# Attention b of a two-attention layer stack: how the row maxima are placed into the queries, and when the other work runs beside it

## The chip, the cores and the metric

The kernel runs on one core of one Trainium2 chip. TensorE (PE) multiplies matrices and transposes; its weight loads are listed apart (PEld). VectorE (DVE), ScalarE (ACT) and GpSimd (POOL) do the elementwise work, and SyncE (SP) issues every transfer, in order, from one queue. The metric is the device time in microseconds. An instruction's line is given as L781 and so on.

## The reference, cut to what matters

Two batches of 512 positions with 512 features pass through four residual layers. All of it is float32.

```python
x = x + attn_a(layernorm(x))      # 32 heads of 128, 8 key/value heads, int4-style weights
x = x + ffn(layernorm(x))         # 8 low-rank experts, two of them chosen per position
x = x + attn_b(layernorm(x))      # 32 heads of 16, 8 key/value heads
x = x + ffn(layernorm(x))         # the same weights as before

# attn_b
q, k = rope(q), rope(k)
att = einsum(q, k) / sqrt(16)                  # per head, (512, 512)
att = where(causal, att, -inf)
probs = softmax(att)                           # needs each row's maximum
out = (probs @ v) @ Wo
```

## The kernel before, in words

Attention a and the first expert layer of batch 0 come first. The change is in what follows, attention b, with the expert layers of both batches running beside it.

**Pairs and steps.** Attention b handles two heads at a time, a *pair*; there are 32 pairs, 16 for each batch. For every pair two generators run. `maxima` (L742) computes the scores with rows on partitions (`sc_b`, L758), adds the causal mask and reduces each row to its maximum on DVE (L762). `probabilities` (L789) computes the scores again, transposed (`st_b`, L805), takes exp on ACT (L811) and clears the upper triangle on POOL (L814). Each has three *steps* per pair: `sc_b` in the order 128+256, 512, 384 columns, and `st_b` as 512, 384, 128+256. `probabilities` runs LEAD = 8 steps behind `maxima`. Pair p has its first maxima step at step 3p.

**How the maximum gets subtracted.** Queries and keys are split into a high and a low float32r part and laid out so that one matmul over 64 partitions gives the whole product. The maximum is appended as two more partitions, 64 and 65: the keys hold -1 there and the queries the maximum's high and low part. So when `maxima` runs, these rows have to be zero, and before `probabilities` runs they have to hold the maxima. Before the change this is done as follows. POOL clears the two rows of a query buffer (L740) when it is loaded again. After the last reduction of a pair, POOL splits the maxima of each head into `mm` (L770, L771), four small operations. `maxima_in` (L776) transposes `mm` on PE into `tpm` (L781, four matmuls), and ACT copies two rows to each head's half of the query buffer (L784, two copies).

**Where the queries come from.** `queries_halved` (L724) splits the queries of four pairs on ACT and POOL into `hl`, and `spread` (L707) writes it twice to DRAM (L711). `queries_in` (L735) loads one pair's 64 rows from there into one of five query buffers (L738). Keys go the same way (`keys_in`, L718).

**The order of the work.** The main loop (L926 on) writes out PE's order by hand: each step places at most one `maxima_in`, one step of `probabilities`, one of `maxima`, two of the products with the values (`num_b`, L831) when they are due, and then side work. The order on the other engines, SP among them, is planned from dependences while the program is built. All `sc_b`, `st_b` and `tpm` tiles share five PSUM buffers, in turn.

**Side work and its pace.** Side work is a chain of generators that yield their cost in units of about one microsecond of PE (0.9 for a 512-column float32 matmul, MM, L157). Each step adds `pace` to a budget and runs side work until the budget is spent. A generator may yield a larger number to hold the work back: `norm_parts` (L158) yields 7.0 between a layer norm's statistics and its transposes. In the first half of the loop the side work is the end of the first expert layer of batch 1 (`py_f`) and batch 1's projections (`pkv_b`, `pq_b`, and the transposes `pxT_b`, `tpk`, `tpq`); in the second half it is the output projection of batch 0 (`po`, L887), the second expert layer of batch 0 and then `po` of batch 1. After the loop the rest of batch 0's second expert layer, the last `po` and the second expert layer of batch 1 run alone. The last `po` waits for the softmax denominators, which pass through DRAM (`dens_b`, `rb_b`).

Of the kernel before, what the change touches and what calls it, by code (L numbers as in the profile page):

```python
# [11 lines left out]
F32 = mybir.dt.float32  # L12
I32 = mybir.dt.int32
F32R = mybir.dt.float32r
AF = mybir.ActivationFunctionType
ALU = mybir.AluOpType
# [3 lines left out]
P = 128  # L20
B, S, DM = 2, 512, 512
# [10 lines left out]
B_NH, B_NKV, B_HD = 32, 8, 16  # L32
# [8 lines left out]
def kernel(  # L41
# [21 lines left out]
    nc = tc.nc  # L63
# [27 lines left out]
    order = const.tile([P, NE], F32, tag="order", name="order")  # L91
# [66 lines left out]
    def norm_parts(b, which):  # L158

        var = small.tile([P, NT, 2], F32, tag="mv", name=f"mv_{which}_{b}")  # L160
        for t in range(NT):
            st = small.tile([P, 6], F32, tag="st", name=f"st_{which}_{b}_{t}")
            nc.vector.bn_stats(st, x[b, t])
            nc.vector.bn_aggr(var[:, t, :], st)
        std = small.tile([P, NT], F32, tag="std", name=f"std_{which}_{b}")
        nc.scalar.activation(std, var[:, :, 1], AF.Sqrt, bias=eps)
        rstd = small.tile([P, NT], F32, tag="rstd", name=f"rstd_{which}_{b}")
        nc.vector.reciprocal(rstd, std)
        yield 7.0
        xT = place("xT", [P, NC, S], f"xnT_{which}_{b}")  # L170
        for t in range(NT):
            xn = place("xn", [P, DM], f"xn_{which}_{b}_{t}")
            nc.vector.tensor_scalar(
                xn, x[b, t], var[:, t, 0:1], rstd[:, t : t + 1], ALU.subtract, ALU.mult
            )
            pt = place("bank", [P, NC, P], f"pxT_{which}_{b}_{t}")
            for c in range(NC):
                nc.tensor.transpose(pt[:, c, :], xn[:, ts(c, P)], ident)
            nc.scalar.copy(xT[:, :, ts(t, P)], pt)
            yield MM  # L180
        return xT
# [98 lines left out]
    with ExitStack() as actx:  # L280
# [221 lines left out]
        for n in range(len(units) + 4):  # L502
# [7 lines left out]
            if at(3):  # L510
                g, b, h, nm = at(3)
# [4 lines left out]
            if at(0):  # L516
                g, b, h, nm = at(0)
# [8 lines left out]
            if at(4):  # L526
                g, b, h, nm = at(4)
                turn.append(output(wo[g], h, g * A_G + h, b, *ats.pop((g, b, h)), nm))
            if at(2):
                g, b, h, nm = at(2)  # L530
# [32 lines left out]
    for sp in range(4):  # L563
        for par in range(2):
            at = sp * STRIP + par * B_HD
# [6 lines left out]

    HALF, HM = P // 2, P // 2 + 2
    NQ = 5
    qs = [w2.tile([P, 2, S], F32, tag=f"qs{n}", name=f"qs_{n}") for n in range(NQ)]
    ks = [w2.tile([P, 4, S], F32, tag=f"ks{n}", name=f"ks_{n}") for n in range(2)]
# [6 lines left out]
    for pad in (*ks, *qs, *vpads, *(mm.bitcast(F32) for mm in mmp)):  # L585
        nc.gpsimd.memset(pad, 0.0)
    for pad in ks:
        nc.gpsimd.memset(pad[HALF:HM], -1.0)
    for pad in vpads:
        for t in range(NT):  # L590
            for kh in range(2):
# [4 lines left out]
    bp = ctx.enter_context(tc.tile_pool(name="b", bufs=1))  # L596
    hp = ctx.enter_context(tc.tile_pool(name="hT", bufs=1))
    hlp = ctx.enter_context(tc.tile_pool(name="hl", bufs=1))
    dram = ctx.enter_context(tc.tile_pool(name="dram", bufs=2, space=bass.MemoryType.DRAM))
    ptp = ctx.enter_context(tc.tile_pool(name="pT2", bufs=5))  # L600
    ps_x = ctx.enter_context(tc.tile_pool(name="ps_x", bufs=5, space=PSUM))
    ps_n = ctx.enter_context(tc.tile_pool(name="ps_n", bufs=1, space=PSUM))
# [30 lines left out]
    qTs, khls = {}, {}  # L633
# [65 lines left out]
    STEPS, LEAD = 3, 8  # L699
# [4 lines left out]

    def spread(hl, nm, order):  # L707

        to = dram.tile([4, P, S], F32, tag=f"spread{nm[0]}", name=f"spread_{nm}")
        for twice in range(2):  # L710
            nc.sync.dma_start(  # L711
                to[order[twice]].rearrange("n r s -> r n s"), hl.bitcast(F32)
            )
        return to.rearrange("n (d h) s -> (n d) h s", h=B_NKV)

    kparts, qparts = {}, {}

    def keys_in(b, kh):  # L718

        if kh == 0:  # L720
            kparts[b] = spread(khls[b], f"k_{b}", (slice(0, 4, 2), slice(1, 4, 2)))
        nc.sync.dma_start(ks[kh][:HALF], kparts[b][:, ts(kh, 4), :])

    def queries_halved(p):  # L724

        b, kh, g, _ = pairs[p]
        hl = hlp.tile([P, 2, S], F32R, tag="hl", name=f"hl_{p}")
        src = qTs[b][:, kh * 2 + g // 2, :]
        nc.scalar.copy(hl[:, 0, :], src)
        nc.gpsimd.tensor_tensor(hl[:, 1, :], src, hl[:, 0, :].bitcast(F32), ALU.subtract)  # L730
        to = spread(hl, f"q_{p}", (slice(0, 2), slice(2, 4)))
        for n in range(4):
            qparts[p + n] = to

    def queries_in(p):  # L735
        _, _, g, pr = pairs[p]
        q = qs[p % NQ]
        nc.sync.dma_start(q[:HALF], qparts.pop(p)[:, ts((g % 2) * 2 + pr, 2), :])  # L738
        if p >= NQ:
            nc.gpsimd.memset(q[HALF:HM], 0.0)  # L740

    def maxima():  # L742

        for p, (b, kh, g, pr) in enumerate(pairs):
            q, k = qs[p % NQ].bitcast(F32R), ks[kh].bitcast(F32R)
            top = small.tile([P, NT, 2], F32, tag="top", name=f"top_{p}")
            for tiles in ((0, 1), (3,), (2,)):
                sc = [
                    ps_x.tile([P, S], F32, tag="x", name=f"sc_b_{p}_{tiles[0]}_{h}")
                    for h in range(2)  # L750
                ]
                parts, at = [], 0
                for i in tiles:
                    n = (i + 1) * P
                    parts += [(i, n, h, sc[h][:, at : at + n]) for h in range(2)]
                    at += n
                for i, n, h, part in parts:
                    nc.tensor.matmul(  # L758
                        part, q[:, h, ts(i, P)], k[:, pr * 2 + h, :n], start=True, stop=True
                    )  # L760
                for i, n, h, part in parts:
                    nc.vector.tensor_tensor_reduce(  # L762
                        part, part, tri[:, S - n :], 1.0, -3e38, ALU.add, ALU.max,
                        top[:, i, h : h + 1],
                    )
                if tiles == (2,):
                    mm = mms[p] = mmp[p % len(mmp)]
                    for h in range(2):
                        at = (1 - h) * HALF
                        nc.gpsimd.tensor_copy(mm[:, :, at], top[:, :, h])  # L770
                        nc.gpsimd.tensor_tensor(  # L771
                            mm[:, :, at + 1], top[:, :, h], mm[:, :, at].bitcast(F32), ALU.subtract
                        )
                yield

    def maxima_in(p):  # L776

        mm = mms.pop(p).bitcast(F32)
        tp = ps_x.tile([P, S], F32, tag="x", name=f"tpm_{p}")
        for t in range(NT):  # L780
            nc.tensor.transpose(tp[:HM, ts(t, P)], mm[:, t, :], ident)  # L781
        for h in range(2):
            at = (1 - h) * HALF
            nc.scalar.copy(qs[p % NQ][HALF:HM, h, :].bitcast(F32R), tp[at : at + 2, :])  # L784


    due = []
# [115 lines left out]
    def parts(stage, n):  # L903
        for _ in range(n):
            next(stage, None)
# [7 lines left out]
    for kh in range(2):  # L913
        keys_in(0, kh)
# [7 lines left out]
    half = total // 2  # L922
    banks[:], homes["we"] = BESIDE, (wep, "we")
    side = chain(later, projections(1))
    pace, left = 1.05, 0.0
    for step in range(total + LEAD):  # L926
        with tc.manual_schedule(engines={mybir.EngineType.PE}):
            if step == half - 8:
                run(side)
                keys_in(1, 0)  # L930
            if step == half - 4:
                side = output_b(0, (0, 1))
                pace, left = 0.38, 0.0
            if step == half + LEAD:
                keys_in(1, 1)
            if step == half + LEAD + 10:
                side = chain(side, output_b(0, (2, 3)), experts(0, "f2", True))
                pace, left = 1.05, 0.0
            if step == total - 6:
                side = chain(output_b(1, (0, 1)), side)  # L940
                pace, left = 1.5, 0.0
            quotients[:] = [q for q in quotients if next(q, None) is not None]
            p, at = divmod(step + 4, STEPS)
            if at == 0 and p % 4 == 3 and p + 1 < len(pairs):
                queries_halved(p + 1)
            if at == 0 and 2 <= p < len(pairs):
                queries_in(p)
            p, at = divmod(step - 4, STEPS)
            if at == 0 and 0 <= p < len(pairs):
                maxima_in(p)  # L950
            if LEAD <= step:
                next(ps)
            if step < total:
                next(ms)

            if len(due) > 1 and due[1][0] <= step:
                for _ in range(2):
                    weighted_b(*due.pop(0)[1])
            left += pace
            while left > 0:  # L960
                got = next(side, None)
                if got is None:
                    left = 0.0
                else:
                    left -= got
# [2 lines left out]
        weighted_b(*due.pop(0)[1])  # L968

    run(*quotients)  # L970
    parts(side, 12)
    run(output_b(1, (2, 3)))
    homes["we"] = ptp, f"pT{S}"
    run(side, experts(1, "f2", True))
# [90 lines left out]
```

## Time and profile before

| | |
|---|---|
| median of 3 runs | 1115.84 us (1114.67 to 1116.47) |
| the profiled execution's own time | 1118.32 us |
| its span, first to last instruction | 1116.6 us |
| granted TensorE clock, mean | 0.985 |
| attention b's loop, first score to the end of its last steps | 807 to about 1052 us |
| PE, DVE, ACT, POOL busy | 95%, 77%, 55%, 53% |

In the profile a group's row has the line, engine, operation, what it writes and reads, its shape and its count; then the busy time and the mean of one, and after the next bar the engine's idle time just before it and what ended that. A timeline row has start, duration, engine, line and operation, and in brackets the idle time before. A row of windows has, for each stretch, the busy time and the number of instructions of PE, PEld, DVE, ACT and POOL, then the granted clock (1.00 is full speed), the share in which the DMA engines are busy, and GB/s. PE's busy time contains waiting inside a stream of matmuls, so 95% is not PE at its peak.

### The profile page before, as it was taken

How to read it: one execution, taken by the hardware profiler on the slowest of the kernel's cores; microseconds unless marked ns; L12 is line 12 of the kernel's file. 1: busy time of each engine (PE TensorE's matmuls, PEld its weight loads, DVE VectorE, ACT ScalarE, POOL GpSimd, SP SyncE). 2: the span in 40 equal slices, each digit the busy share in tenths (PEclk: the TensorE clock that was granted, in tenths of full speed). 3: DMA queues.
4: the chain of work that ended last, by engine and by line, in shares of the span. 5: the costliest groups of instructions: out<-in, count | busy, mean ns of one | idle time of the engine just before them, and what ended most of it. 6: DMA issues, size and time to landing. Idle time of an engine off the chain costs nothing.

```text
span 1116.6 us, 16186 instructions
## 1 busy us (share of the span) xinstructions
PE 1065.4 (95%) x4940; PEld 712.1 (64%) x4940; DVE 863.6 (77%) x2175; ACT 616.9 (55%) x1421; POOL 587.4 (53%) x916
## 2 busy tenths in 40 slices
PE   5799999999999999999999999999989999999988
PEld 3467677777777777777777777555467555555534
DVE  6889899999999999999999889573376667667142
ACT  3556566566566566566556665513166667575410
POOL 2556556656756756756656666261245566454200
PEclk9899999999999999999999999999989999889999
DMA  7301010021010010010121000043342245211010
GB/s 288 114 1 38 1 38 24 16 76 51 26 39 5 34 38 5 35 38 1 39 76 38 1 1 1 1 153 85 96 135 82 60 143 146 57 47 34 21 44 38
DMA packets 23270, 60.47 MB, mean 54 GB/s; under 512 B 4368, under 2 KB 5328, under 8 KB 20368
## 3 DMA queue, kind: packets, MB, share of 16 engines
q1 hardware_dynamic: 23184, 59.44, 16.4%
q8 instruction: 40, 0.66, 0.2%
q14 instruction: 46, 0.38, 0.1%
HBM read 45.53 MB, written 12.85 MB: 52 GB/s over the span
## 4 chain that ended last, share of the span: by engine, by line
PE 79%; DVE 10%; ACT 3%; POOL 3%; issue 2%; DMA 2%; SPq 0%; ACTq 0%; DVEq 0%; POOLq 0%
PE av L429 11%; PE sc L396 10%; PE tp L424 5%; PE ps_o L439 5%; PE ps_o L438 5%; PE ps_q L358 5%; PE ph_f L207 5%; PE ps_q L359 4%; PE py_f L266 4%; PE num_b L831 4%; PE st_b L805 3%; PE sc_b L758 3%; PE pq_b L678 2%; PE po L887 2%; DVE r_q L365 2%
## 5 line engine op out<-in xcount | busy, mean ns | idle before, releaser
L404 ACT ACTIVATE p<-sc,nmx 128x128 f32<-128x128 f32 (+3 forms) x256 | 135.7, 530 | 95.5 <-DVE nmx L399 92.7
L376 POOL TENSOR_TENSOR r_q<-r_q,tab 128x512 f32<-128x512 f32 x64 | 82.5, 1288 | 190.9 <-DVE rs_q L375 190.9
L396 PE MATMUL sc<-kT,qT 128*128 128x128 f32 (+3 forms) x512 | 180.2, 433 | 0.9 <-POOL qT L377 0.9
L365 DVE SCALAR_TENSOR_TENSOR r_q<-ps_q,s_q,r_q 128x512 f32<-128x512 f32 x192 | 143.5, 748 | 37.3 <-PE ps_q L359 23.5
L413 POOL TENSOR_SCALAR p<-p,rden 128x128 f32<-128x128 f32 (+3 forms) x256 | 140.2, 561 | 59.1 <-DVE rden L411 20.7
L425 ACT COPY pT<-tp 128x128 f32<-128x128 f32 (+3 forms) x256 | 109.4, 428 | 104.4 <-PE tp L424 103.8
L762 DVE CUSTOM_DVE_ANT_0 sc_b<-sc_b,tri 128x128 f32<-128x128 f32 (+3 forms) x256 | 119.6, 517 | 51.9 <-PE sc_b L758 44.7
L429 PE MATMUL av<-pT,v 128*128 128x512 f32 (+3 forms) x512 | 148.5, 433 | 0.0
L429 PEld LDWEIGHTS av<-pT,v 128*128 128x128 f32 x512 | 97.0, 190 | 80.2 <-issue 53.9
L448 DVE SCALAR_TENSOR_TENSOR acc<-ps_o,s_o,acc 128x512 f32<-128x512 f32 x186 | 137.4, 739 | 5.5 <-PE ps_o L439 5.4
L399 DVE CUSTOM_DVE_ANT_0 sc<-sc,tri 128x128 f32<-128x128 f32 (+3 forms) x256 | 125.3, 490 | 8.0 <-PE sc L396 7.1
L358 PE MATMUL ps_q<-xh,w_q 128*128 128x512 f32 x256 | 123.9, 484 | 7.4 <-DVE r_q L365 7.3
L424 PE MATMUL tp<-ident,p 128*128 128x128 f32 x640 | 113.1, 273 | 2.6 <-POOL p L413 2.6
L811 ACT ACTIVATE pT_b<-st_b 128x384 f32<-128x384 f32 (+1 forms) x192 | 90.5, 528 | 40.4 <-PE st_b L805 39.4
L396 PEld LDWEIGHTS sc<-kT,qT 128*128 128x128 f32 x512 | 96.0, 189 | 24.8 <-POOL qT L377 1.3
L438 PE MATMUL ps_o<-ah,w_o 128*128 128x512 f32 x256 | 107.9, 422 | 1.7 <-DVE acc L448 1.0
L439 PE MATMUL ps_o<-al,w_o 128*128 128x512 f32 x256 | 104.9, 410 | 3.4 <-DVE al L152 3.4
L424 PEld LDWEIGHTS tp<-ident,p 128*128 128x128 f32 x640 | 83.1, 141 | 30.6 <-issue 6.4
L359 PE MATMUL ps_q<-xl,w_q 128*128 128x512 f32 x256 | 102.0, 398 | 0.0
L814 POOL TENSOR_SCALAR_AFFINE_SELECT pT_b<-pT_b 128x128 f32<-128x128 f32 (+1 forms) x192 | 62.9, 338 | 64.2 <-ACT pT_b L811 61.7
L377 POOL TENSOR_TENSOR qT<-r_q,rs_q 128x512 f32<-128x512 f32 x64 | 85.3, 1333 | 1.0
L446 POOL TENSOR_TENSOR acc<-acc,part 128x512 f32<-128x512 f32 x62 | 79.7, 1286 | 10.1 <-ACT part L445 10.1
(179 smaller groups left out, 2048.6 us busy)
## 6 DMA issues: line engine op xcount, KB each, us to landing
codes_q<-in_q_codes_dram SPq DMA_DIRECT2D x8, 1024.0 KB
codes_o<-in_o_codes_dram SPq DMA_DIRECT2D x8, 1024.0 KB
spread_q<-hl SPq DMA_DIRECT2D x16, 512.0 KB
qs<-spread_q SPq DMA_DIRECT2D x32, 256.0 KB
x_a<-in_x_dram SPq DMA_DIRECT2D x8, 256.0 KB
codes_k<-in_k_codes_dram SPq DMA_DIRECT2D x2, 1024.0 KB
codes_v<-in_v_codes_dram SPq DMA_DIRECT2D x2, 1024.0 KB
x_r<-in_x_dram SPq DMA_DIRECT2D x8, 256.0 KB
```

What stands on the lines that cost most here:

```text
L358: nc.tensor.matmul(ps, w[:, c, ts(h, A_HD)], xh[b][:, c, :], start=True, stop=False)
L359: nc.tensor.matmul(ps, w[:, c, ts(h, A_HD)], xl[b][:, c, :], start=False, stop=True)
L365: nc.vector.scalar_tensor_tensor(r, ps, s, r, ALU.mult, ALU.add)
L396: nc.tensor.matmul(sc[:, :n], qT[:, ts(i, P)], kT[:, :n], start=True, stop=True)
L399: nc.vector.tensor_tensor_reduce(sc[:, :n], sc[:, :n], tri[:, S - n :], -(A_HD**-0.5), 3e38, ALU.add, ALU.min, nmx,)
L404: nc.scalar.activation(pr, sc[:, :n], AF.Exp, bias=nmx, scale=-1.0, accum_out=den[:, i % 2 : i % 2 + 1],)
L413: nc.gpsimd.tensor_scalar(prs[j], prs[j], rden[:, j % 2 : j % 2 + 1], 1.0, ALU.mult, ALU.mult)
L424: nc.tensor.transpose(tp[:, j, :], prs[i][:, ts(j, P)], ident)
L429: nc.tensor.matmul(av[:, j * P :], v[:, j, :], pT[:, j, j * P :], start=(j == 0), stop=(j == NT - 1))
L438: nc.tensor.matmul(ps, w[:, h, ts(n, P)], ah, start=True, stop=False)
L439: nc.tensor.matmul(ps, w[:, h, ts(n, P)], al, start=False, stop=True)
L448: nc.vector.scalar_tensor_tensor(to, ps, s, to, ALU.mult, ALU.add)
```

## The change

The maxima take four partitions instead of two (HM is 68 instead of 66): high and low part of both heads. The keys of even heads have -1 in the first two of these rows and 0 in the others, those of odd heads the reverse. Thus one cast and one subtraction on POOL split both heads, and one copy on ACT puts all four rows under both heads. A query load brings 68 rows: the four at the end of each DRAM buffer are written once with zeros, so that POOL no longer clears anything. The DRAM buffers are two for the queries and one for the keys, made once. `maxima_in` comes one step later. The norm's hold falls from 7.0 to 3.0, the paces change, the first queries of batch 1 are split at step 44 with the first keys instead of at 41, and after the loop 16 yields of side work instead of 12 run ahead of the last `po`.

```diff
@@ norm_parts
-        yield 7.0
+        yield 3.0
@@
-    HALF, HM = P // 2, P // 2 + 2
+    HALF, HM = P // 2, P // 2 + 4
...
-        nc.gpsimd.memset(pad[HALF:HM], -1.0)
+        for h in range(2):
+            nc.gpsimd.memset(pad[HALF:HM, h : 4 : 2, :], -float(h))
+            nc.gpsimd.memset(pad[HALF : HALF + 2, h : 4 : 2, :], h - 1.0)
...
-    def spread(hl, nm, order):
-        to = dram.tile([4, P, S], F32, tag=f"spread{nm[0]}", name=f"spread_{nm}")
-        for twice in range(2):
-            nc.sync.dma_start(
-                to[order[twice]].rearrange("n r s -> r n s"), hl.bitcast(F32)
-            )
-        return to.rearrange("n (d h) s -> (n d) h s", h=B_NKV)
+    kspread = dram.tile([HALF * B_NKV, S], F32, tag="kspread", name="kspread")
+    qspread = [
+        dram.tile([HM * B_NKV, S], F32, tag=f"qspread{n}", name=f"qspread_{n}") for n in range(2)
+    ]
+    for to in qspread:
+        nc.sync.dma_start(to[HALF * B_NKV :], qs[0][: (HM - HALF) * B_NKV, 0, :])
+
+    def spread(to, hl, parts):
+        to = to[: HALF * B_NKV].rearrange("(n r) s -> n r s", r=P)
+        for part in parts:
+            nc.sync.dma_start(to[part].rearrange("n r s -> r n s"), hl.bitcast(F32))
+
+    def spread_heads(to):
+        return to.rearrange("(r h) s -> r h s", h=B_NKV)
@@ queries_in
-        q = qs[p % NQ]
-        nc.sync.dma_start(q[:HALF], qparts.pop(p)[:, ts((g % 2) * 2 + pr, 2), :])
-        if p >= NQ:
-            nc.gpsimd.memset(q[HALF:HM], 0.0)
+        at = (g % 2) * 2 + pr
+        nc.sync.dma_start(qs[p % NQ][:HM], spread_heads(qspread[p // 4 % 2])[:, ts(at, 2), :])
@@ maxima
-                    for h in range(2):
-                        at = (1 - h) * HALF
-                        nc.gpsimd.tensor_copy(mm[:, :, at], top[:, :, h])
-                        nc.gpsimd.tensor_tensor(
-                            mm[:, :, at + 1], top[:, :, h], mm[:, :, at].bitcast(F32), ALU.subtract
-                        )
+                    high, low = mm[:, :, HALF:HM:2], mm[:, :, HALF + 1 : HM : 2]
+                    nc.gpsimd.tensor_copy(high, top)
+                    nc.gpsimd.tensor_tensor(low, top, high.bitcast(F32), ALU.subtract)
@@ maxima_in
-        for h in range(2):
-            at = (1 - h) * HALF
-            nc.scalar.copy(qs[p % NQ][HALF:HM, h, :].bitcast(F32R), tp[at : at + 2, :])
+        both = tp[HALF:HM].unsqueeze(1).to_broadcast([HM - HALF, 2, S])
+        nc.scalar.copy(qs[p % NQ][HALF:HM].bitcast(F32R), both)
@@ the loop
-    pace, left = 1.05, 0.0
+    pace, left = 0.8, 0.0
...
-            if step == half - 8:
+            if step == LEAD:
+                pace = 0.95
+            if step == half - 4:
                 run(side)
                 keys_in(1, 0)
-            if step == half - 4:
+                queries_halved(len(pairs) // 2)
                 side = output_b(0, (0, 1))
-                pace, left = 0.38, 0.0
+                pace, left = 0.37, 0.0
...
                 side = chain(side, output_b(0, (2, 3)), experts(0, "f2", True))
-                pace, left = 1.05, 0.0
+                pace, left = 0.95, 0.0
             if step == total - 6:
                 side = chain(output_b(1, (0, 1)), side)
-                pace, left = 1.5, 0.0
+                pace, left = 1.4, 0.0
...
-            if at == 0 and p % 4 == 3 and p + 1 < len(pairs):
+            if at == 0 and p % 4 == 3 and p + 1 < len(pairs) and p + 1 != len(pairs) // 2:
                 queries_halved(p + 1)
...
-            p, at = divmod(step - 4, STEPS)
+            p, at = divmod(step - 5, STEPS)
             if at == 0 and 0 <= p < len(pairs):
                 maxima_in(p)
@@ after the loop
-    parts(side, 12)
+    parts(side, 16)
```

## The prediction

> **What bounds the kernel now.** I read the page's shares first, then its clock row. All times are from the profiled execution's start.
>
> ```profile
> PE 1065.4 (95%) x4940; PEld 712.1 (64%) x4940; DVE 863.6 (77%) x2175; ACT 616.9 (55%) x1421; POOL 587.4 (53%) x916
> ...
> PEclk9899999999999999999999999999989999889999
> ```
>
> PE (TensorE) is busy 95% of the span, and the chain that ended last runs 79% over it. The clock row dips in slices 30, 35 and 36, all in attention b. The changed lines run after 740 us, so I cut attention b into stretches: first steps, side work in the first half, few side units, second half. The columns are busy time of PE, weight loads, DVE, ACT and POOL, the granted clock and the DMA share.
>
> ```profile
> 807.00:830.00 23.00, 19.82 (x74) 13.60 (x75) 19.24 (x75) 11.83 (x21) 8.47 (x25) 0.78 0.42 137
> 830.00:902.00 72.00, 69.89 (x456) 45.60 (x454) 47.14 (x188) 48.23 (x106) 42.50 (x116) 1.00 0.30 86
> 902.00:952.00 50.00, 47.81 (x306) 28.26 (x306) 34.07 (x133) 35.86 (x74) 33.28 (x95) 1.00 0.51 154
> 952.00:1024.00 72.00, 68.63 (x404) 40.62 (x405) 49.52 (x193) 43.71 (x86) 33.95 (x104) 0.91 0.15 44
> ```
>
> The second stretch is PE's own. The first is DVE's (19.2 of 23) and ran at a clock of 0.78; the third is nobody's, PE waiting briefly for each of the others; the fourth lost clock. The same view around two of the drops:
>
> ```profile
> 949.40:952.80 3.40, 2.55 (x10) 1.41 (x10) 2.35 (x8) 2.69 (x6) 2.16 (x6) 1.00 0.61 164
> 952.80:959.60 6.80, 6.07 (x29) 2.69 (x27) 3.77 (x16) 2.02 (x4) 2.66 (x8) 0.50 0.14 43
> ...
> 1062.00:1065.40 3.40, 0.72 (x2) 0.30 (x2) 1.38 (x2) 0.00 (x0) 0.00 (x0) 1.00 0.56 214
> 1065.40:1068.80 3.40, 3.33 (x5) 0.96 (x4) 0.69 (x1) 0.00 (x0) 0.00 (x0) 0.51 0.02 9
> ```
>
> A thin 3.4 us of PE is followed by half clock for 3.4 or 6.8 us. In the loop this happened at 819.7 (10.2 us), 952.8 (6.8) and 983.5 (6.8): 23.8 us at half speed, worth at most 11.9. Then the rows that the diff touches, from the groups by shape:
>
> ```profile
> L784 ACT CAST qs<-tpm 2x512 fp32r<-2x512 f32 x64 | 36.8, 575 | 30.3 <-PE tpm L781 29.7
> ...
> L740 POOL MEMSET qs<- 2x1024 f32 x27 | 25.8, 956 | 24.6 <-PE st_b L805 24.5
> L781 PE MATMUL tpm<-ident,mm 128*66 128x128 f32 x128 | 21.0, 290 | 4.9 <-POOL mm L771 4.4
> ...
> L771 POOL TENSOR_TENSOR mm<-top,mm 128x4 fp32r<-128x4 f32 x64 | 14.1, 220 | 4.0
> ```
>
> PE stood still for 4.9 us before the transposes `tpm`, for POOL's `mm`. POOL's own 24.6 us before the clearing are waits with affine selects queued behind them.
>
> **The change, part by part.**
>
> *Clearing and splitting on POOL.* 27 memsets of 0.956 us go, and 128 small operations (0.22 and 0.20 us) become 64: 25.8 + 13 = 39 us off POOL, about 1.2 a pair. POOL is at 0.6 to 0.67 in the loop, so this shortens latency only. `mm` is ready 0.4 us sooner and `tpm` comes a step (about 2 us) later, so its wait should go. Where DVE was late anyway the wait returns at the next score tile: I take 70% of 4.9, **-3.4** (ends -4.9 and 0).
>
> *One ACT copy.* 2 x 575 ns become one copy of 4x1024. From the exps' 492 and 599 ns for 384 and 512 columns (0.84 ns a column), 1024 cost 599 + 512 x 0.84 = 1.03 us: 0.12 us less a pair, hidden under PE. But it now stands in front of the two 512-wide exps, in the step with ACT's largest load: 0 (-0.1 to +0.3 a pair, so -3 to +10). I take the low part, because ACT idles 29.7 us waiting for `tpm`: it has room.
>
> *Setup.* Four clearings of 4 or 2 rows per key tile replace one of 2.0 us: at 0.95 us per 1024 columns +3.6 us of POOL, under the 9.6 us that POOL idles before `rot_kb` at 763. Two short zero transfers join SP's queue at about 758, 15 us ahead of the next one. 0; without that cover 3.6.
>
> *The query loads have 68 rows instead of 64.* By bytes alone this is 6%: 0.1 us of a load. The Trainium skill's page "DMA: Bandwidth & Descriptors", section "Why a DMA increments its semaphore by 16 and not by 1", speaks against it: a transfer from SP's queue runs on the largest number of engines up to 16 that divides its outer dimension, so 64 rows get 16 engines and 68 get 4. This trace has such a case: the 4-row `dens_b` transfer issued at 837.20 has five updates of its semaphore, one at 838.18 and four from 838.85 to 838.94; the 64-row load issued at 826.22 has sixteen, from 829.03 to 829.72. I follow the rule. A load then has 17 packets of 4 KB on an engine instead of 4. They took 0.16 us each at best and 0.27 on average where three loads ran together; 13 x 0.18 = 2.3 us more, 5.8 us a load where the typical one takes 3.5.
>
> Most loads hide that: they are issued 7.5 to 13 us ahead of their pair's first matmul (939.44 for 946.95 is the shortest). Two do not. The first load is issued at 803.49, lands at 807.12, and PE starts pair 0 at 807.26 with 0.29 us of idle: **+2.3** (0.1 by bytes, 4.0 with a chilled clock).
>
> *The second half's first queries.* Their split moves from step 41 to 44 and the last query transpose from 39 to 41. Before:
>
> ```profile
> 902.62 0.89 SPq L711 DMA_DIRECT2D spread_q<-hl  x2
> 907.25 0.47 SPq L738 DMA_DIRECT2D qs<-spread_q  x1
> 909.78 0.55 SPq L847 DMA_DIRECT2D dens_b<-o_b  x1
> ```
>
> The ACT split began at 900.60, the load landed at 910.73 and was needed at 915.09 (step 48): 4.4 us to spare. In the changed order the split comes two steps later on ACT, behind step 42's exps, 4 us at about 2 us a step. So the slack is gone at 16 engines, and on 4 PE waits 1.9 to 2.9 us, with score tiles, DVE and ACT queued behind. With a chilled clock for half the cases: **+3.0** (0 to +6.3, that is 2.9 + half of 6.8).
>
> *Other work's paces.* The norm's hold falls from 7 to 3 units, so the projections start one step earlier with four transposes in place by step 11 (one before), the side work fills steps 40 and 41, which were empty, and the second half's norm leaves three empty steps instead of four. About three empty steps fewer. The pair from 946.95 to 952.38 shows what one costs: no other work, 5.43 us for score groups that the timeline starts 0.36 to 0.57 us apart where nothing waits, 3.4 in sum, so 0.5 to 0.7 us of waiting a step: **-1.5** (0 to -3). The pace in the first 8 steps falls from 1.05 to 0.8, but those are DVE's. Fewer thin windows mean fewer drops; the sqrt table loads (1.28 us twice on ACT) remain in both norms and still make one. Of the 11.9 us I take a quarter, **-3.0** (-8 to +2).
>
> *The tail.* Four more yields put `py_f_0_3` ahead of the last `po`:
>
> ```profile
> 1051.92 10.46 PE L266 MATMUL py_f<-lora_b,hT_f 128*128 128x512 f32 x24
> 1065.06 9.02 PE L887 MATMUL po<-wo,oN_b 128*128 128x512 f32 x16 [2.67 <-issue]
> 1073.92 3.60 PE L266 MATMUL py_f<-lora_b,hT_f 128*128 128x512 f32 x8
> 1078.76 2.02 PE L178 MATMUL pxT_f<-ident,xn_f 128*128 128x128 f32 x16 [1.24 <-DVE xn_f L173]
> ```
>
> Its 3.44 us cover the 2.67 us wait for `rb_b`. `po` then starts at 1065.85; its second matmul meets `oN_b` at 1066.76, and the eight end at 1072.8. The norm behind is now uncovered: DVE's four rounds of add, stats and aggregate (1.72 us each) from 1067.75 end at 1074.5, sqrt and the `py` add take 0.7, xn 0.6: `pxT_f` at 1076.0 instead of 1078.76, -2.8. PE idles 3.1 us before it. The skill's page "TensorE: Matmul & The Clock Gate", Part 1, lets the clock drop after an idle window of some 3.4 us; by that the gain is 2.8. In the rows above a gap of 2.67 us was enough, and in the loop 0.77 + 0.73 were. I follow the trace: a drop 7 times in 10, worth 1.6: **-1.7** (-2.8 to 0).
>
> **Sum.** -3.4 + 2.3 + 3.0 - 1.5 - 3.0 - 1.7 = -4.3. The profiled execution took 1118.3 us (span 1116.6 and 1.7 around it), so 1114.0; it lies 2.5 above the median, so the median goes from 1115.8 to **1111.5**.
>
> **Rivals.** *Slower: late loads decide.* The loads on four engines keep PE waiting and each wait chills the clock: start +4.0, step 48 +6.3, and two of the loads around 939 to 949, whose lead is 7.5 us, late by 1.4 each because SP also holds the `dens` chain: +13.1. Against it stand -3.4, -1.5 and -1.7, and no gain of clock: +6.5, **1122.3**. It decides once a load takes over about 7 us. For it: SP's waits of 68.8 us before its loads. Against: most leads are over 9.5 us.
>
> *Nothing gained.* The waits removed return as waits for score tiles, since DVE and ACT are at 0.7 beside them: `mm` -1.0, spreading -0.5, tail -1.7, start +2.3, the switch hidden: -0.9, **1114.9**. For it: the second stretch is PE's whatever the order.
>
> *The loads keep 16 engines.* Then 2.3 and 2.6 fall away: **1106.6**. Against it: the five updates above.
>
> **How the numbers follow.** About 0.2% (2.2 us) is what a measurement tells from no change: 1113.6 to 1118.1. The likeliest case has 0.50 (own range 1107 to 1115.5): 0.43 faster, 0.07 same. Late loads 0.22 (1117 to 1128): 0.19 slower, 0.03 same. Nothing gained 0.20 (1112.5 to 1118.5): 0.03 faster, 0.14 same, 0.03 slower. Sixteen engines 0.08, faster. Together 0.54, 0.24, 0.22. The range runs from the sixteen-engine case's 1104 to 1121.5, in the middle of the late loads.
>
> **What would show it.** A query load with five semaphore updates and about 5.8 us to landing; PE idle about 2.5 us before pair 0's first score and 2 us before pair 16's; no idle time before `tpm` for `mm`; `pxT_f` of the last norm about 13.5 us after `py_f_0_2` ends instead of 16.4. The prediction is wrong if the clock drops more than twice in the loop, if ACT's copy delays the exps so that pairs in the third stretch take more than 6.25 us on average (902.42 to 952.38 for eight), or if loads land in 3.5 us.

## The result, and the profile after

The changed kernel takes 1125.62 us (median of six runs, 1121.81 to 1130.52) where the kernel before takes 1115.18. The ratio is 1.0099, 95% interval 1.0073 to 1.0125; the two medians alone lie 10.4 us apart. So it is 10 to 11 us **slower**. The forecast was 1111.5 in a range of 1104 to 1121.5, with 0.54 on faster, so sign and range were both wrong.

The page of the changed kernel, shares and clock row:

```profile
PE 1058.7 (94%) x4940; PEld 710.7 (63%) x4940; DVE 862.7 (77%) x2175; ACT 609.8 (54%) x1389; POOL 552.9 (49%) x831
...
PEclk8999999999999999999999999999989999889999
```

POOL and ACT have less to do, as was forecast (587.4 and 616.9 before), and the span is 1124.0 us instead of 1116.6. Cut into the same pairs as before (pairs 0 to 3, 4 to 13, 14 to 21, 22 to 30, then pair 31 and the tail), the view of stretches reads:

```profile
808.00:834.58 26.58, 18.64 (x76) 12.94 (x77) 18.91 (x75) 11.65 (x18) 5.85 (x15) 0.81 0.27 100
834.58:908.88 74.30, 70.85 (x454) 47.07 (x453) 48.61 (x192) 45.27 (x94) 30.37 (x91) 0.98 0.29 86
908.88:965.24 56.36, 48.85 (x306) 29.55 (x305) 33.95 (x133) 33.98 (x66) 22.53 (x66) 0.95 0.37 122
965.24:1035.43 70.19, 66.57 (x408) 40.14 (x408) 47.35 (x189) 42.44 (x78) 22.55 (x76) 0.94 0.18 60
1035.43:1124.00 88.57, 81.53 (x315) 40.16 (x314) 30.26 (x76) 22.99 (x42) 11.04 (x30) 1.00 0.10 34
```

The same five stretches took 22.56, 72.60, 49.96, 71.76 and 92.46 us before; the first and the third of them there:

```profile
807.26:829.82 22.56, 19.64 (x72) 13.39 (x73) 19.24 (x75) 11.65 (x20) 8.29 (x25) 0.78 0.42 137
...
902.42:952.38 49.96, 47.39 (x306) 28.06 (x305) 34.03 (x133) 35.75 (x73) 32.93 (x95) 1.00 0.51 155
```

So 4.0, 1.7 and 6.4 us were lost in the first three, 1.6 and 3.9 won in the last two. The net 6.6 us are less than the 10.4 between the medians, because the profiled execution of before took 1118.32 us, 3.1 above its median. PE's idle time from just before the first score of pair 0 to that of pair 31 rose from 10.9 to 24.8 us. Five places hold 14.9 us of it, in the timeline of PE:

```profile
808.00 0.70 PE L763 MATMUL sc_b<-ks,qs 128*128 128x128 f32 x4 [2.25 <-issue]
...
828.80 0.80 PE L806 MATMUL st_b<-qs,ks 128*128 128x128 f32 x2 [5.69 <-DVE top L767]
...
905.21 0.60 PE L783 MATMUL tpm<-ident,mm 128*68 128x128 f32 x4 [2.78 <-DVE top L767]
...
923.58 0.70 PE L763 MATMUL sc_b<-ks,qs 128*128 128x128 f32 x4 [1.92 <-DMA qs<-qspread]
...
957.70 0.62 PE L806 MATMUL st_b<-qs,ks 128*128 128x384 f32 x2 [2.25 <-ACT qs L785]
```

The first (pair 0) and the fourth (pair 16) are the two waits for a query load that the prediction priced (for the first the profile names no releaser, but the load landed at 807.91). The other three are not, and they are the larger part, 10.7 us. The groups by shape that answer to those shown of before:

```profile
L785 ACT CAST qs<-tpm 4x1024 fp32r<-4x1024 f32 x32 | 32.1, 1004 | 49.9 <-PE tpm L783 49.7
...
L783 PE MATMUL tpm<-ident,mm 128*68 128x128 f32 x128 | 20.4, 283 | 2.8 <-DVE top L767 2.8
...
L775 POOL TENSOR_TENSOR mm<-top,mm 128x8 fp32r<-128x8 f32 x32 | 6.5, 203 | 2.4
...
L738 ACT CAST hl<-qT 128x512 fp32r<-128x512 f32 x8 | 5.0, 620 | 30.1 <-DMA qspread<-hl 30.1
```

In the kernel before, the last of them was:

```profile
L729 ACT CAST hl<-qT 128x512 fp32r<-128x512 f32 x8 | 5.0, 621 | 13.6 <-DMA spread_q<-hl 13.6
```

The wide copy takes 1.00 us and `tpm` no longer waits for POOL. What grew is the last row: ACT stood 30.1 us (13.6 before) in front of the cast into `hl`, because the transfer that still read the old `hl` had not ended. What that does at the start is in the chain that ended last, in its part from 802 to 828 us (start, duration, what):

```profile
802.32 0.63 ACT hl L738
802.95 0.07 issue
803.01 1.27 POOL hl L739
804.29 0.02 issue
804.30 0.39 SPq L722
804.69 0.04 issue
804.74 0.47 SPq L722
805.21 0.04 issue
805.25 14.35 DMA qs<-qspread
...
820.11 5.41 DMA qspread<-hl
...
825.62 0.62 ACT hl L738
826.24 0.02 issue
826.26 1.28 ACT L166
...
827.55 0.30 ACT std_b L166
...
827.88 0.04 DVE rstd_b L168
...
828.00 0.30 DVE sc_b L767
```

Pair 3's query load took 14.35 us. Only then could the halves of pairs 8 to 11 overwrite that DRAM tile (5.41 us), and only then could ACT fill `hl` for pairs 12 to 15. Everything else of ACT was queued behind this cast: the norm's square root, its two table loads and the exps. DVE in turn had the norm's reciprocal, which needs that root, in front of the row maxima that PE waited for. PE stood 5.69 us, and its clock was halved from 823.9 for 10.2 us.

Why did a load take 14 us, and why did transfers that are not loads slow down too? The updates of the semaphores, in us (a load of 68 rows shows one about 0.4 us after its issue and four at its end):

```
issued   transfer        updates of its semaphore
802.27   qs (68 rows)    802.70 | 807.49 to 807.91 (4)
802.63   qs (68 rows)    803.07 | 810.20 to 811.48 (4)
802.94   qs (68 rows)    803.43 | 812.88 to 813.92 (4)
804.30   hl (128 rows)   806.90 to 807.04 (12) | 814.16 to 815.19 (4)
805.25   qs (68 rows)    805.78 | 818.06 to 819.60 (4)
```

A load of 68 rows ends on four engines. The halves in `hl` go out over sixteen: twelve were done at 807.04, the other four 8 us later, after the three loads issued ahead. **While a narrow transfer runs, it holds up the wide ones queued behind it**, since a wide one is not done before its share on those same four engines is. The Trainium skill's page "DMA: Bandwidth & Descriptors" has both halves of this. Besides the count of engines it says that such a transfer takes the lowest-numbered of them (section "Why a DMA increments its semaphore by 16 and not by 1"). It also says that each engine takes its work in the order of its ring (section "Queues, rings and completion order"). No view here numbers the engines, but the split of the sixteen updates into twelve and a late four agrees. The prediction used the count alone.

The third place, pair 13, is the same with another victim. The timeline of DVE:

```profile
902.15 0.75 DVE L878 TENSOR_TENSOR oN_b<-oN_b,rb_b 128x512 f32<-128x512 f32 x1 [2.42 <-DMA rb_b<-dens_b]
903.47 0.69 DVE L878 TENSOR_TENSOR oN_b<-oN_b,rb_b 128x512 f32<-128x512 f32 x1 [0.57 <-DMA rb_b<-dens_b]
904.08 0.29 DVE L767 CUSTOM_DVE_ANT_0 sc_b<-sc_b,tri 128x128 f32<-128x128 f32 x1
```

A query load issued at 894.82 landed at 900.79; the two `rb` broadcasts behind it, 5.74 and 6.28 us under way (4.46 and 5.50 before), held DVE in front of the row maxima, and with them `tpm` by 2.78 us. The broadcasts also started late: the transfer they wait for (`dens_b<-sums_b`, on sixteen engines) went out at 893.23 behind a load issued at 890.15 and took 3.10 us instead of 1.46. At the fifth place ACT again stood before a cast into `hl` (timeline of ACT):

```profile
956.00 0.62 ACT L738 CAST hl<-qT 128x512 fp32r<-128x512 f32 x1 [5.46 <-DMA qspread<-hl]
956.64 1.00 ACT L785 CAST qs<-tpm 4x1024 fp32r<-4x1024 f32 x1
```

### The profile page after: what moved, and what is told of

It reads as the page before. It is cut to its first block, busy times and chain, and to the rows that moved or that the text cites. A ratio compares the mean times of both kernels' runs of the same rounds, so it can differ in the third digit from the quotient of the medians.

```text
span 1124.0 us, 15995 instructions
## 1 busy us (share of the span) xinstructions
PE 1058.7 (94%) x4940; PEld 710.7 (63%) x4940; DVE 862.7 (77%) x2175; ACT 609.8 (54%) x1389; POOL 552.9 (49%) x831
## 4 chain that ended last, share of the span: by engine, by line
PE 80%; DVE 7%; DMA 6%; ACT 2%; issue 2%; POOL 1%; SPq 1%; ACTq 0%; DVEq 0%; POOLq 0%
PE av L429 12%; PE sc L396 11%; PE tp L424 6%; PE ps_o L439 5%; PE ps_o L438 5%; PE ps_q L358 5%; PE ph_f L207 5%; PE ps_q L359 5%; PE py_f L266 3%; PE st_b L806 3%; PE sc_b L763 3%; PE num_b L832 3%; PE pq_b L681 2%; PE po L888 2%; DMA qspread<-hl 2%; DMA qs<-qspread 2%
## 5 line engine op out<-in xcount | busy, mean ns | idle before, releaser
L806 PE MATMUL st_b<-qs,ks 128*128 128x256 f32 (+3 forms) x256 | 79.6, 410 | 11.2 <-DVE top L767 6.3
```

## The experiments

Three theories were put to the test: *four engines* (the narrow loads and what queues behind them), *paces* (the other work's new order thins PE's work) and *maxima* (the wide copy and the later `tpm` hold the score tiles). Times are medians; ratios are to the kernel before on the same chip (1115.2 to 1115.9 us), with 95% intervals, and are not quite the quotients of the medians.

| kernel | us | ratio | interval |
|---|---|---|---|
| changed kernel | 1125.6 | 1.0099 | 1.0073 to 1.0125 |
| rows80 | 1109.4 | 0.9944 | 0.9929 to 0.9959 |
| before_rows68 | 1153.9 | 1.0352 | 1.0315 to 1.0389 |
| hl2 | 1125.1 | 1.0099 | 1.0061 to 1.0136 |
| paces_alone | 1107.1 | 0.9926 | 0.9900 to 0.9952 |
| rows80_maxima | 1115.7 | 1.0004 | 0.9987 to 1.0021 |
| tail_alone | 1113.6 | 0.9977 | 0.9964 to 0.9991 |
| first80 | 1119.8 | 1.0033 | 1.0020 to 1.0046 |
| rows80_step4 | 1105.2 | 0.9906 | 0.9873 to 0.9939 |
| idle57 | 1117.8 | 1.0015 | 1.0004 to 1.0025 |
| idle64 | 1108.7 | 0.9931 | 0.9908 to 0.9954 |
| rows80_step4_5 | 1107.9 | 0.9925 | 0.9906 to 0.9944 |
| rows70_step4 | 1108.1 | 0.9926 | 0.9907 to 0.9945 |

### The loads on sixteen engines (rows80)

```diff
-    HALF, HM = P // 2, P // 2 + 4
+    HALF, HM, HL = P // 2, P // 2 + 4, P // 2 + 16
...
-        nc.sync.dma_start(qs[p % NQ][:HM], spread_heads(...)[:, ts(at, 2), :])
+        nc.sync.dma_start(qs[p % NQ][:HL], spread_heads(...)[:, ts(at, 2), :])
```

(The DRAM tiles and their rows of zeros grow from HM to HL too.)

> The changed kernel, with query loads of 80 rows instead of 68: the 12 added rows are zeros, so the result is the same, but 80 divides by 16 and 68 only by 4. Three theories for the +11 us. FOUR ENGINES: the 68-row load sits on four DMA engines for 5 to 14 us, the split halves `hl` that go out to DRAM queue behind it on the same engines, and ACT, which must not overwrite `hl`, stands in front of everything else. Then a load takes 3.5 to 4.5 us again, the gap of 5.69 us in pair 3 is under 1 us, ACT waits under 1 us for `hl` inside the loop, and the time is 1109 to 1114. PACES: the other work at new paces leaves thin windows, so the clock drops: 1122 to 1127, pair 3 still over 10 us. MAXIMA: the one wide ACT copy and the step later hold the score tiles: 1122 to 1127.

Measured: 1109.4 us, 16.2 below the changed kernel, although every load moves 18% more bytes. Most of *four engines* came: a load takes 3.49 us at the median instead of 5.92, pairs 0 to 3 take 21.66 us instead of 26.58. Two signs of it missed: PE's gap in pair 3 is 1.07 us, not under 1, and ACT still waits more than 1 us for `hl` inside the loop (1.63 at 939.93). ACT's waits for `hl` and DVE's for the broadcasts, of the changed kernel first and then of this one (us in total, times, longest; over 800 to 1090 us):

```profile
ACT hl L738 <- DMA qspread<-hl: 30.1, 5, 13.6
...
DVE oN_b L878 <- DMA rb_b<-dens_b: 6.6, 6, 2.4
DVE oN_b L878 <- DMA dens_b<-oN_b: 5.2, 1, 5.2
```

```profile
ACT hl L738 <- DMA qspread<-hl: 15.4, 3, 8.1
...
DVE oN_b L878 <- DMA rb_b<-dens_b: 4.1, 4, 2.3
```

The 5.2 us in the changed kernel are DVE's wait up to 960.91; it too ended with a broadcast, which landed at 960.72, though the profile names another transfer. Of the 15.4 us, 13.7 are at the start, where the casts stand at 802.85 and 811.59, as they did before (13.6); there ACT has little else to do. *Paces* and *maxima* as causes of the loss fall with this run: both are still in this kernel, and it is 0.56% faster than the one before.

### The narrow loads in the kernel before (before_rows68)

```diff
-        nc.sync.dma_start(q[:HALF], qparts.pop(p)[:, ts((g % 2) * 2 + pr, 2), :])
+        nc.sync.dma_start(q[: HALF + 4], spread_heads(qspread[p // 4 % 2])[:, ts(at, 2), :])
         if p >= NQ:
             nc.gpsimd.memset(q[HALF:HM], 0.0)
```

(The two standing DRAM tiles with their rows of zeros are added too.)

> The kernel before with nothing changed but its query loads: 68 rows instead of 64, out of two standing DRAM tiles whose last rows are zeros; POOL's clearing, the two ACT copies, paces and order stay. FOUR ENGINES: five semaphore updates per load, ACT stands several us for `hl`, a gap of 2 to 6 us in pairs 2 to 4, and 1120 to 1128. PACES or MAXIMA: at most the 2.3 us that pair 0 waits for its first load, 1115 to 1118.

Measured: 1153.9 us, 38 above before, far over even the *four engines* figure. The waits tell why:

```profile
POOL qs L751 <- DMA qs<-qspread: 38.4, 19, 5.5
...
PE tpm L792 <- POOL mm L782: 27.2, 20, 3.7
ACT hl L739 <- DMA qspread<-hl: 19.9, 2, 14.3
```

POOL's clearing may only run once the load has landed, and the split of `mm` is queued behind it. With narrow loads this makes `tpm` late in 20 pairs. Clearing by the load itself, as the change does, takes POOL out of that line; in the changed kernel the 68 rows cost 16 to 17 us instead of 38.

### Two buffers for the halves (hl2)

```diff
-    hlp = ctx.enter_context(tc.tile_pool(name="hl", bufs=1))
+    hlp = ctx.enter_context(tc.tile_pool(name="hl", bufs=2))
```

> The changed kernel with two buffers for the split halves `hl` instead of one; the loads keep 68 rows. FOUR ENGINES, if the damage goes by way of ACT waiting to overwrite `hl`: the loads still take 5 to 14 us, but ACT no longer waits in front of std and the exps, pair 3's gap falls below 1.5 us, and the time is 1114 to 1120. If the late loads hold PE directly: 1123 to 1127 with the gaps before the scores as they were. PACES or MAXIMA: 1122 to 1127, pair 3's gap unchanged.

Measured: 1125.1 us, no gain, and yet pair 3 fell from 12.32 to 7.56 us with the 5.69 us gap gone. The waits of this kernel:

```profile
DVE oN_b L878 <- DMA rb_b<-dens_b: 11.4, 5, 6.0
ACT hl L738 <- DMA qspread<-hl: 8.5, 3, 5.1
```

So ACT's wait was what made that gap, but not what sets the end. Five narrow loads now stand in one burst (the last lands 15.5 us after its issue), PE waits 3.76 us instead of 2.25 at pair 0, and DVE waits up to 6.0 us for a broadcast, which costs 4.50 us at pair 21. This expectation came true in its mechanism and missed in its time: with one victim gone, the four engines find another.

### Which loads (first80)

```diff
+        n = HL if p < NQ else HM
-        nc.sync.dma_start(qs[p % NQ][:HL], spread_heads(...)[:, ts(at, 2), :])
+        nc.sync.dma_start(qs[p % NQ][:n], spread_heads(...)[:n, ts(at, 2), :])
```

(The diff is against rows80.)

> The changed kernel with 80 rows (16 engines) in the first five query loads only; the other 27 keep 68 rows on four engines. It splits the 16.2 us between the changed kernel and its 80-row version. By the traces the two part by 6.5 us up to pair 5 and by about 10 after it: 1118 to 1120. If only the burst at the start hurts: 1109 to 1112, pairs 13, 16 and 20 as short as with 80 rows. If the start is nothing and the second half all: 1124 to 1126.

Measured: 1119.8 us, as expected. By the ratios the first five loads cost 7.4 us (1.0099 to 1.0033) and the other 27 cost 9.9 us (1.0033 to 0.9944): 17.3 together, 16.2 by the medians; by the intervals each part is good to 2 or 3 us. The waits at pairs 13 and 20 are still there (2.42 before `tpm`, 1.20 before `st_b`).

### Transfers that nothing waits for (idle57, idle64)

```diff
     def maxima_in(p):
+        nc.sync.dma_start(idle[p][:57], qs[p % NQ][:57])
```

The base is rows80; `idle` is 32 DRAM tiles that are never read. The control has 64 in both places.

> The changed kernel with 80-row loads, and 32 added transfers that nothing waits for: at each pair's `tpm` the first 57 rows of its queries go out to a DRAM tile of their own that is never read. 57 is 3 times 19, so by the rule of the outer dimension they sit on three engines, 19 packets each, about 5 us. QUEUEING (what other transfers lose behind a narrow one is what decides): 3 to 10 us above the 80-row kernel's 1109.4, so 1112 to 1120, with the spreads of `hl` and the `rb` broadcasts longer. OWN LATENESS (a narrow transfer harms only who waits for it): 1108.5 to 1111, and the same as its control with 64 rows.

> The control: the same 32 transfers that nothing waits for, with 64 rows, so on 16 engines with 4 packets each; the bytes are 12% more, the place in SP's queue is the same. QUEUEING: 1109 to 1112, at least 3 us below the 57-row kernel. OWN LATENESS: 1108.5 to 1111, equal to it. If it is SP's time for issuing and waiting that costs, both are slower alike, 1112 to 1118.

Measured: 1117.8 and 1108.7 us. The 57-row transfers show four updates, three of them with data, and take 6.4 us at the median; those of 64 rows show sixteen and 3.6 us. With 12% more bytes and the same places in SP's queue the wide ones cost nothing, the narrow ones 9.1 us. The `rb` broadcasts took 6.15 us behind narrow transfers, 4.97 behind wide ones, 4.37 without either. DVE's waits for them, narrow and then wide:

```profile
DVE oN_b L881 <- DMA rb_b<-dens_b: 13.2, 6, 5.8
```

```profile
DVE oN_b L881 <- DMA rb_b<-dens_b: 7.2, 5, 3.6
```

Being in the way is enough: no engine but SP waits for these transfers. The two traces show where the time goes. Pair 12 takes 11.79 us behind narrow transfers and 7.66 behind wide ones, pairs 28 and 29 together 19.76 and 14.73. In pair 12 a 57-row transfer was issued at 889.87 and landed at 895.91; a broadcast, which runs on eight engines, followed at 890.22. Five of the eight were done at 893.90; the last three, as many as the narrow transfer takes, came from 896.36 to 897.23, and PE stood 3.96 us behind DVE.

(SP also waits for an older transfer before it takes up that one's semaphore again. It stood 63.4 us in front of the narrow transfers and 44.5 in front of the wide ones, and the second broadcast of pair 12 was issued 2.45 us after the first instead of 1.28. So part of the 9.1 us goes by SP's queue; how much was not separated.)

### The other parts alone (paces_alone, tail_alone, rows80_maxima)

```diff
@@ paces_alone: the kernel before with
-        yield 7.0
+        yield 3.0
...  (new paces, the switch at step 44, halves for the second batch there)
-    parts(side, 12)
+    parts(side, 16)
@@ tail_alone: the kernel before with
-    parts(side, 12)
+    parts(side, 16)
@@ rows80_maxima: rows80 with all of paces_alone put back, tpm still at step - 5
```

> The kernel before with only the other work's order of the change: hold 3 instead of 7, the new paces, the switch at step 44, 16 parts in the tail; the maxima, their clearing, the loads of 64 rows and the step of `tpm` are those of before. FOUR ENGINES: this is the change without its loss, 1108 to 1114. PACES: 1121 to 1127, clock drops beyond four. MAXIMA: 1108 to 1114 too.

> The kernel before with one number changed: 16 parts instead of 12 ahead of the last output projection. PREDICTION'S STEP: -2.8 without a drop of the clock, -1.7 with one 7 times in 10, so 1112.5 to 1114. TRACE OF THE CHANGED KERNEL (from pair 31 to the end 88.6 us instead of 92.5, no drop at 1065): -3.9, so 1111 to 1112. If the tail gained only together with the loop: 1115 to 1116.

> The changed kernel with 80-row loads (16 engines) and all of the other work's order put back: hold 7, old paces, the switch at steps 40 and 44, the halves for the second batch at step 41, 12 parts in the tail. What is left of the change is the maxima's part: rows cleared by the load, 8 columns split at once, one ACT copy, `tpm` a step later. PREDICTION'S STEP: the 4.9 us that PE waits for `mm` go at 70%, -3.4, so 1111 to 1113. NOTHING: the 80-row kernel with all parts came out 2.3 us above the one with only the order changed, so the maxima's part is worth zero or costs a little, 1115 to 1119, with the waits for `mm` gone and as much waiting elsewhere.

Measured: 1107.1, 1113.6 and 1115.7 us. Taken by the ratios, the order of the other work is worth -8.3 us (-11.2 to -5.4), of which the tail is -2.6 (-4.0 to -1.0). The maxima's part on sixteen engines is worth +0.4 (-1.4 to +2.3), that is nothing. *Paces* fell, and of *maxima* this remains: PE's waits for `mm` are nearly gone, and it waits as much elsewhere, 12.3 us of idle time in the loop against 10.9 in the kernel before.

### The step of `tpm`, and what beats both kernels (rows80_step4, rows80_step4_5, rows70_step4)

```diff
-            p, at = divmod(step - 5, STEPS)
+            p, at = divmod(step - 4, STEPS)
```

This is rows80 with one step less, and rows70_step4 has loads of 70 rows in it.

> The changed kernel with 80-row loads and the maxima's transposes `tpm` at the step of the kernel before, one step earlier. If the later step is what moves ACT's copy in front of the wide exps, where the second norm's table loads stand too (pair 26 takes 11.7 us with a drop of the clock, 7.3 us in the kernel with only the order changed): 1104 to 1107. If the later step is worth something, because `mm` is then always ready: 1110 to 1114, with waits of 0.4 to 1.4 us for `mm` back. No difference: 1108.5 to 1110.

> The kernel with 80-row loads and `tpm` at the step of before, measured again with five rounds, as the candidate that beats both: 1104 to 1107. If its first time was luck, it comes back to the 80-row kernel's 1109.

> The same with loads of 70 rows. By the rule of the outer dimension 70 runs on 14 engines, 5 packets each: fifteen semaphore updates, 3.3 to 4.2 us a load, and 1104 to 1107 like 80 rows. If anything that isn't a multiple of 16 falls to a few engines: five updates or fewer and 1116 to 1122.

Measured: 1105.2 us in four executions, 1107.9 in six of the same kernel, and 1108.1 with 70 rows. The first figure was partly luck: against rows80 (0.9944) the longer run's 0.9925 is no difference that the intervals separate. Loads of 70 rows show fifteen updates, fourteen with data, and the first takes 3.88 us: so 70 rows are spread over fourteen engines though 70 is no multiple of 16. All three, like paces_alone, are faster than both kernels, about 0.75% below the one before and 1.7% below the changed one; among them the runs don't tell which is best.

## Why the prediction was wrong

Its sum had six terms and -4.3 us. The runs give them so:

| term | predicted | measured |
|---|---|---|
| `tpm` no longer waits for `mm`; one ACT copy | -3.4 | +0.4 (rows80_maxima) |
| paces and clock drops | -4.5 | -5.7 (paces_alone less tail_alone) |
| tail | -1.7 | -2.6 (tail_alone) |
| narrow loads: first load and step 48 | +5.3 | +16 to +17 (changed kernel less rows80) |

Added up, the measured rows give 8 to 9 us, where 10 to 11 were measured in all; what is left is no more than the intervals allow. That the second row agrees is partly luck. The prediction had -1.5 for the paces and -3.0 for fewer clock drops; the profile of paces_alone has 6.8 us at half clock in the loop, just as that of tail_alone, and is 3.6 us shorter there all the same (209.5 us against 213.1).

**The step that failed is "The query loads have 68 rows instead of 64", in its words "Most loads hide that" and "Two do not."** It got the count of engines, the five updates and the duration right (5.8 us predicted, 5.92 at the median, 4.73 at the least), and both waits that it named are there: 2.25 us at pair 0 (2.3 predicted, 2.5 in its list of signs) and 1.92 at pair 16 (1.9 to 2.9), and no third. These two are 4.2 us of PE's time; the loads cost 16 to 17. The prediction looked only for who waits for the loads. It did not ask who shares their engines: the halves in `hl`, whose buffer ACT must have back before it does anything else, and the `rb` broadcasts, for which DVE stands in front of the maxima. idle57 against idle64 shows that transfers which no engine but SP waits for can cost 9 us in this way. The prediction's estimate of 0.18 us a packet also took a load by itself; in the burst at the start each narrow load holds the four engines for about 3 us (landings at 807.91, 811.48, 813.92), and they add up.

**The first term was the second miss.** The 4.9 us before `tpm` were counted at 70%. They went, and came back as other waits; rows80_maxima shows nothing left. The rival "nothing gained" had given the reason, DVE and ACT at 0.7 beside PE, and allowed 1.0.

**The rival "late loads decide"** said 1122.3 (1117 to 1128) and held the result, with the right part of the change as its cause. Its mechanism was only half right: it had loads late at PE around 939 to 949, where the trace has the halves late at ACT (956.00) and with them the exps. The threshold that it named, a load of over about 7 us, was passed by eight of the 32 loads, three of them in the burst at the start, and not by the typical one.

**What held.** POOL's saving is real and hidden. ACT's copy takes 1.00 us (1.03 predicted) and delays nothing that shows. The tail gained -2.6 us, with the predicted -1.7 inside its interval: the last norm's `pxT_f` comes 13.2 us after `py_f_0_2` (13.5 predicted, 16.4 before; 24 of the 28 matmuls in the first row, so it ends at about 1072.9), with 1.45 us idle before it instead of 3.1, and no drop of the clock, where 7 in 10 were given to one (of the eleven profiles with this tail only tail_alone's has it, at 1072.6):

```profile
1062.42 12.18 PE L266 MATMUL py_f<-lora_b,hT_f 128*128 128x512 f32 x28
1075.36 1.10 PE L888 MATMUL po<-wo,oN_b 128*128 128x512 f32 x2 [0.76 <-PE py_f L266]
1076.61 6.28 PE L888 MATMUL po<-wo,oN_b 128*128 128x512 f32 x14 [0.15 <-DVE oN_b L878]
1082.72 1.88 PE L266 MATMUL py_f<-lora_b,hT_f 128*128 128x512 f32 x4
1086.05 2.03 PE L178 MATMUL pxT_f<-ident,xn_f 128*128 128x128 f32 x16 [1.45 <-DVE xn_f L173]
```

Of the signs that would prove the prediction wrong, two came: four clock drops in the loop (823.9, 905.8, 960.4, 994.5) instead of two, and a third stretch of 56.36 us for eight pairs, 7.05 each and over the 6.25 allowed. Not for the reason given there, ACT's copy: rows80 has the same copy and takes 6.26.

## What to carry to other kernels

Price a narrow transfer twice: once at whoever waits for it, and once at every transfer that is queued behind it on the same engines, with the in-order engine that waits for *that*. Before adding a few rows to a transfer, look at the divisors of its outer dimension: 80 rows were faster than 68, and 70 as good as 80. And when a wait is taken away beside engines that are two thirds busy, don't count on its gain: here 4.9 us of waiting went and nothing was won.

## What the runs showed of the hardware that was not expected

A transfer over sixteen engines can be three quarters done for 8 us: twelve updates of the `hl` transfer issued at 804.30 came by 807.04, the last four from 814.16 on.

The drops of the clock in one profiled execution are a poor guide to the code. tail_alone has in attention b's loop the instructions of the kernel before, in the same order on every engine; its profile has 6.8 us at half clock there and 213.1 us from pair 0 to pair 31, where the profile of before has 23.9 us and 216.9. A forecast that reads a gain out of the drops of one trace, as the -3.0 here, rests on a number that moves by more than that from one execution to the next.
